# Layer 0 of a four-layer network on one Trainium2 core: one scan of 1024 per pair of states instead of two of 512, and half of softplus's additions as matmuls

## The chip, the cores and the metric

The kernel runs on one core of a Trainium2 chip. Its time is the device time of one execution in microseconds (us), median of several runs; lower is better. The engines of a core work side by side, each on its own queue of instructions in order: TensorE (PE in the profile; PEld is its weight load), VectorE (DVE), ScalarE (ACT), GpSimd (POOL) and SyncE (SP), which here only issues DMAs. They wait for each other through semaphores.

## What is computed

An image batch `x` of 8 x 96 x 64 x 64 (f32) goes through four layers, each `x = x + layer(group_norm(x))`. The change touches the first alone, a selective state space layer (Mamba) over the 4096 pixels of an image, with 192 inner channels and 16 states per channel. The channel flip of the reference leaves the scan itself as it is:

```python
xz = seq @ in_proj_w.T
u, res = jnp.split(xz, 2, axis=-1)
uc = conv_general_dilated(u, conv_w, ...)      # causal, 4 taps, per channel
u = silu(uc)
dbc = u @ x_proj_w.T
dt, B, C = jnp.split(dbc, [DT_RANK, DT_RANK + D_STATE], axis=-1)
delta = softplus(dt @ dt_proj_w.T + dt_proj_b)
dA = exp(delta * A)
dBu = delta * B * u
state_t = dA_t * state_(t-1) + dBu_t           # 192 x 16 states, 4096 steps
y_t = sum over states of state_t * C_t
y = (y + u * D) * silu(res)
out = y @ out_proj_w.T
```

Layer 1 is a Fourier-domain layer, layer 2 a second state space layer (four directions), layer 3 a deformable convolution.

## The kernel before

**Tiling.** `layer0` cuts each image into 8 chunks of NW = 512 pixels, 64 chunks in all. The 192 channels are two halves of HD = 96. A *group* is 32 channels times 4 states on the 128 partitions, and two such sets of states, a *pair*, side by side in one tile of 128 x 2 x 512. A chunk has 12 groups: for each half `h`, six groups `e`. Each takes one *slot* of time `t`; chunk number n starts at slot T = 12 n, and slots are spoken of modulo 12.

**A group's work.** `dd` (delta and delta times u, broadcast by a DMA from SBUF to 128 partitions, six slots ahead, every second group); `da` = exp(delta A) in PSUM tile `ps_d`, two ACT operations of 512 (L405), one slot ahead; `dbu` = (delta u) B on POOL (L424), two slots ahead; the recurrence as `tensor_tensor_scan` on DVE, two of 512 with the starting value from `carry` (L747), in place in `ps_d`; the product with C back into `dbu`, on DVE one slot later (L433); the sum over states by two matmuls into `ps_y` (L444, `total`). For a *late* group the scan writes into `dbu` instead, POOL multiplies by C (L430), and `ps_d` is free as soon as the scan is done; LATE0 names them. After each group ACT copies the last column of both scans into `carry` (L756, `keep`) for the next chunk.

**Order.** `Slots.slot` writes the instruction stream slot by slot. For slot t: the `dd` DMA of t+6; the two exps of t+1; side work marked "first"; the first scan of t; the total of t-2; "pe" side work and the late total of t-4; "act" side work; `dbu` of t+2; "pool" side work; a late product of t-2 on POOL; the product of t-1 on DVE; the second scan of t; then "dve", "sp" and "end" side work. Engines follow that order strictly. Side work is placed by slot number relative to a chunk's T: `sl.at(T - 24, "act", silu)`.

**Side work of a chunk**, before its first group: the convolution as eight matmuls into `ps_a`, one PSUM bank shared by all side matmuls (`inner`, L647); two gate matmuls; four copies to `raw` (L674); one silu over 96 x 2048 with a table load before and one after (L685, L686); `low` (delta's rank, B and C, L691) and its copy; the store of B and C rows to DRAM and their broadcast back, `brep` and `crep`; softplus in `Slots.steps`, as max(x, 0) + log(1 + e) with e = exp(-|x|) and a term for what rounding of 1 + e lost: Abs, Relu, Exp, +1, Ln, -1 on ACT and `add`, `lost`, `delta`, then `delta_u`, on POOL, each over both halves (96 x 1024). After the last group: `y_out`, `gated` (POOL, L798), the output matmuls (L808), the residual as an identity matmul (L815), statistics, store.

**Buffers.** `ps_d` has three buffers of two banks, `ps_y` and `ps_a` one bank each, `dbu` a ring of 7.

Of the kernel before, what the change touches and what calls it, by code (L numbers as in the profile page):

```python
# [39 lines left out]
class Names:  # L40


    def __init__(self):
        self.n = 0
# [271 lines left out]
class Plan:  # L316


    def __init__(self, S):
        self.S, self.plan = S, {}  # L320
# [4 lines left out]
    def put1(self, base, name, i, run):  # L325
        t, engine = PLAN2[name][i]
        self.at(base + t, engine, run)
# [16 lines left out]
class Group:  # L344


    def __init__(self, **kw):
        self.__dict__.update(kw)


class Slots(Plan):
# [14 lines left out]
    def __init__(self, S, consts, pool, psd, ring, red=None):  # L366
        super().__init__(S)
# [22 lines left out]
    def slot(self, t):  # L390
# [19 lines left out]
        if g:  # L410
            g.h = g.dbu if g.late else g.da
            g.scan[0](g.h, g.da, g.dbu)
# [7 lines left out]
        self.side(t, "act")  # L420
        g = G(t + 2)
# [12 lines left out]
        g = G(t)  # L434
        for scan in g.scan[1:] if g else ():
            scan(g.h, g.da, g.dbu)
# [14 lines left out]

    def steps(self, T, out, f, pre, u, reset):


        nc, S, st = self.S.nc, self.S, {}

        def first(h):
            def pe():
                st["p"] = pre(h)

            def act():
                if h == 0:
                    st["e"] = new(f, [HD, 2, NW], "sp_e")
                    st["m"] = new(f, [HD, 2, NW], "sp_m")
                nc.scalar.activation(st["e"][:, h, :], st["p"], AF.Abs)
                nc.scalar.activation(st["m"][:, h, :], st["p"], AF.Relu)

            self.at(T - 20 + h, "pe", pe)
            self.at(T - 19 + h, "first", act)

        first(0)
        first(1)

        def exp():
            nc.scalar.activation(st["e"], st["e"], AF.Exp, scale=-1.0)

        def one():
            st["w"] = new(f, [HD, 2, NW], "sp_w")
            nc.scalar.activation(st["w"], st["e"], AF.Identity, bias=S.one[:HD])

        def ln():
            st["s"] = new(f, [HD, 2, NW], "sp_s")
            nc.scalar.activation(st["s"], st["w"], AF.Ln)

        def less():
            nc.scalar.activation(st["w"], st["w"], AF.Identity, bias=self.minus[:HD])

        for n, run in enumerate((exp, one, ln, less)):
            self.at(T - 18 + n, "act", run)

        def add():
            nc.gpsimd.tensor_tensor(st["m"], st["m"], st["s"], ALU.add)

        def lost():
            nc.gpsimd.tensor_tensor(st["w"], st["w"], st["e"], ALU.subtract)

        def delta():
            out["d"] = new(f, [HD, 2, 2, NW], "delta", bufs=2)
            nc.gpsimd.tensor_tensor(out["d"][:, :, 0, :], st["m"], st["w"], ALU.subtract)

        def delta_u():
            d = out["d"]
            for uv, dv, ov in u(d[:, :, 0, :], d[:, :, 1, :]):
                nc.gpsimd.tensor_tensor(ov, dv, uv, ALU.mult)
            if reset is not None:
                v = d[:, :, 0, :].rearrange("p m (n l) -> p m n l", l=16)
                nc.gpsimd.memset(v[:, :, :, reset : reset + 1], FAR)

        for n, run in enumerate((add, lost, delta, delta_u)):
            self.at(T - 15 + 2 * n, "pool", run)  # L510

# [49 lines left out]
def layer0(S, src, dst, st_in, st_out, images):  # L561
    tc, nc = S.tc, S.nc
    with ExitStack() as ctx:
# [26 lines left out]
        sl = Slots(S, cp, wp, psd, RING0)  # L590
# [48 lines left out]
        def chunk(im, b, c, T):  # L639
            ch, at = {}, c * NW  # L640

            def inner(h, k0, k1):
                def run():
                    if k0 == 0:
                        ch["ps"] = new(psa, [128, NW], "ps_a")
                    for k in range(k0, k1):
                        nc.tensor.matmul(  # L647
                            ch["ps"][:HD, :],
                            wk[:, k, h * HD : (h + 1) * HD],
                            im["xn"][:, at + k : at + k + NW],  # L650
                            start=k == 0,
                            stop=k == 3,
                        )

                return run
# [14 lines left out]
            def raw(n):  # L670
                def run():
                    if n == 0:
                        ch["raw"] = new(fp, [HD, 4, NW], "raw")
                    nc.scalar.activation(  # L674
                        ch["raw"][:, n, :],
                        ch["ps"][:HD, :],
                        AF.Identity,
                        bias=convb[:, n : n + 1] if n < 2 else 0.0,
                    )

                return run

            def silu():
                ch["ug"] = new(fp, [HD, 4, NW], "ug", bufs=4)
                nc.scalar.activation(ch["ug"], ch["raw"], AF.Silu)  # L685
                nc.scalar.preload_act_table_set(LOG_EXP)  # L686
# [16 lines left out]
            sl.at(T - 34, "pe", inner(0, 0, 2))  # L703
            sl.at(T - 33, "pe", inner(0, 2, 4))
            sl.at(T - 32, "first", raw(0))
            sl.at(T - 29, "pe", inner(1, 0, 4))
            sl.at(T - 28, "first", raw(1))
            for h in range(2):
                sl.at(T - 28 + h, "pe", gate(h))
                sl.at(T - 27 + h, "first", raw(2 + h))  # L710
            sl.at(T - 24, "act", silu)
            sl.at(T - 23, "pe", low)
            sl.at(T - 22, "first", low_out)
            sl.at(T - 22, "sp", low_store)

            def pre(h):
                ps = new(psa, [128, NW], "ps_a")
                nc.tensor.matmul(
                    ps[:HD, :],
                    dtw[:, h * HD : (h + 1) * HD],  # L720
                    ch["low"][: RK + 1, :],
                    start=True,
                    stop=True,
                )
                return ps[:HD, :]

            sl.steps(T, ch, fp, pre, lambda d, du: [(ch["ug"][:, 0:2, :], d, du)], None)

            def spread(name, what, t):
# [10 lines left out]
                sl.at(t, "sp", run)  # L740

            spread("b", 0, T - 9)
            spread("c", 1, T - 6)

            def scan_of(n):
                def scan(out, da, dbu, i):
                    nc.vector.tensor_tensor_scan(  # L747
                        out[:, i, :], da[:, i, :], dbu[:, i, :],
                        carry[:, n + i : n + i + 1] if c else 0.0, ALU.mult, ALU.add,
                    )  # L750

                return [lambda *v, i=i: scan(*v, i) for i in range(2)]
# [19 lines left out]
            def y_out(h):  # L772
                def run():
                    if h == 0:
                        ch["yg"] = new(fp, [HD, 2, NW], "yg", bufs=2)
# [7 lines left out]
            for h in range(2):  # L783
                for e in range(NG):
# [6 lines left out]
                        y=y_of(h, e), scan=scan_of(n), late=c % 2 == 0 and NG * h + e in LATE0,  # L791
# [3 lines left out]
                sl.at(T + h * NG + 7, "act", y_out(h))  # L795
# [32 lines left out]
            sl.at(T + 17, "pool", gated)  # L828
            sl.at(T + 17, "sp", residual)
            sl.at(T + 22, "pe", out(0))  # L830
            sl.at(T + 23, "pe", out(1))
            sl.at(T + 23, "pe", plus)
            sl.at(T + 24, "first", sum_out)
            sl.at(T + 25, "dve", stats_out)
            sl.at(T + 25, "sp", store)
# [425 lines left out]
def layer2(S, src, dst, st_in, st_out, images, cp, W, ready, finish):  # L1261
# [3 lines left out]
    with ExitStack() as ctx:  # L1265
# [13 lines left out]
        sl = Slots(S, cp, wp, psd, RING, W["red"])  # L1279
# [383 lines left out]
        def direction(ch, pr, xs, k, n, T):  # L1663
# [49 lines left out]
            for h in range(2):  # L1713
                for i in range(6):
# [6 lines left out]
                        y=y_of(h, e), scan=[scan], late=24 * (n // 2) + 12 * h + e in LATE2,  # L1721
# [636 lines left out]
```

## Time and profile before

| | us |
|---|---|
| three runs | 17171.51, 17232.79, 17279.42 (median 17232.79) |
| profiled execution | 17209.55 |
| its span, first to last instruction | 17207.5 |
| first scan of layer 0 begins | 99.49 |
| last scan of layer 0 begins | 2832.34 |
| first matmul of layer 1 | 2857.52 |

Busy time of the engines over the whole span: DVE 15501.4 us (90%), POOL 14565.0 (85%), PE 14200.8 (83%), ACT 10161.0 (59%). Line numbers (L747) are those of the kernel before. A line of the order-of-time view is: start, length of one record or of several merged, engine, line, operation, tile written and tiles read, shape, count, and in brackets how long the engine stood idle before it and what released it. A line of the waits is: who waited for whom, total us, times, longest.

### The profile page before, as it was taken

The page shows a single profiled execution, that of the slowest core. Times are in us where ns is not written, and L with a number is a line of the kernel's source. Part 1 is how long each engine was busy: PE and PEld are TensorE (multiplying, and loading weights), DVE is VectorE, ACT ScalarE, POOL GpSimd, SP SyncE. Part 2 cuts the span into 40 slices and gives each one's busy share as a digit, 9 for nine tenths or more (in the row PEclk, how much of TensorE's full clock was granted, in tenths as well). Part 3 has the DMA queues.
Part 4 walks back from the last instruction along what each step waited for, and adds up shares of the span by engine and source line. Part 5 has one row for each costly group of instructions (what it writes and reads, how often), then busy time and mean ns, then how long its engine had stood idle before and what let it go on. Part 6 is the DMA issues. An engine that isn't in the chain of part 4 may idle for free.

```text
span 17207.5 us, 127943 instructions
## 1 busy us (share of the span) xinstructions
PE 14200.8 (83%) x36170; PEld 5621.8 (33%) x36170; DVE 15501.4 (90%) x9787; ACT 10161.0 (59%) x15654; POOL 14565.0 (85%) x8237
## 2 busy tenths in 40 slices
PE   8999998979999999999999999999999444444332
PEld 2333334723333333333333333333333111111111
DVE  7999998679999999999999999999999567677677
ACT  7778775557777777777777777777776211111110
POOL 7999995059999999999999999999999556565555
PEclk9999999989999999999999999999999766666666
DMA  5666664366666666666666666666666444454444
GB/s 123 141 136 137 138 137 94 59 167 144 145 142 146 145 140 148 144 141 148 140 144 147 141 145 146 139 147 144 141 147 142 113 140 145 138 150 141 142 126 123
DMA packets 768532, 2373.66 MB, mean 138 GB/s; under 512 B 255989, under 2 KB 257730, under 8 KB 684265
## 3 DMA queue, kind: packets, MB, share of 16 engines
q1 hardware_dynamic: 620361, 1912.33, 50.9%
q0 software_dynamic: 147456, 453.13, 9.0%
q8 instruction: 285, 4.67, 0.1%
q14 instruction: 430, 3.52, 0.1%
HBM read 1249.81 MB, written 108.66 MB: 79 GB/s over the span
## 4 chain that ended last, share of the span: by engine, by line
PE 36%; issue 12%; DVE 11%; another core or an unknown queue 9%; ACT 7%; POOL 5%; DMA 0%; DVEq 0%; SPq 0%; POOLq 0%; ACTq 0%
PE ps_y L444 17%; DVE ps_d L1691 5%; PE ps_a L1342 5%; PE ps_a L1617 4%; ACT ps_d L405 3%; DVE dbu L433 3%; POOL dbu L424 3%; PE ps_a L2022 2%; DVE v L2205 1%; PE ps_a L1433 1%; PE ps_a L1809 1%; DVE s L2214 1%; POOL dbu L430 1%; PE ps_a L1756 1%
## 5 line engine op out<-in xcount | busy, mean ns | idle before, releaser
L424 POOL TENSOR_TENSOR dbu<-dd,brep 128x1024 f32<-128x1024 f32 x3840 | 9060.2, 2418 | 7.2 <-PE ps_y L444 6.9
L444 PE MATMUL ps_y<-dbu,k_red 128*96 128x512 f32 x15360 | 7192.4, 599 | 281.3 <-DVE dbu L433 229.5
L405 ACT ACTIVATE ps_d<-dd,l_alog 128x512 f32<-128x512 f32 x7680 | 5285.2, 691 | 1425.1 <-DVE dbu L433 1010.2
L1691 DVE TENSOR_TENSOR_SCAN ps_d<-ps_d,dbu 128x1024 f32<-128x1024 f32 x2560 | 5829.2, 2285 | 40.5 <-issue 16.4
L433 DVE TENSOR_TENSOR dbu<-ps_d,crep 128x1024 f32<-128x1024 f32 x3296 | 3981.0, 1208 | 0.1
L444 PEld LDWEIGHTS ps_y<-dbu,k_red 128*96 128x96 f32 x15360 | 2444.8, 163 | 4522.4 <-issue 3402.6
L2187 POOL DMA_INDIRECT v<-t,idx x2304 | 2191.8, 951 | 1523.8 <-DVE s L2214 710.2
L2214 DVE TENSOR_REDUCE s<-v 128x864 f32<-128x3456 f32 x256 | 1553.9, 6070 | 402.3 <-remote 293.8
L747 DVE TENSOR_TENSOR_SCAN ps_d<-ps_d,carry,dbu 128x512 f32<-128x512 f32 x1296 | 1610.7, 1279 | 24.1 <-ACT ps_d L405 17.3
L2205 DVE TENSOR_TENSOR v<-v,ps_w 128x3456 f32<-128x3456 f32 x256 | 958.4, 3744 | 679.9 <-ACT ps_w L2197 571.6
L430 POOL TENSOR_TENSOR dbu<-dbu,crep 128x1024 f32<-128x1024 f32 x544 | 1321.2, 2429 | 5.5 <-DVE dbu L1691 3.2
L2233 ACT COPY smp<-ps_t 128x768 f32<-128x768 f32 (+1 forms) x512 | 244.8, 530 | 1635.1 <-remote 929.0
L1691 DVE TENSOR_TENSOR_SCAN dbu<-ps_d,dbu 128x1024 f32<-128x1024 f32 x512 | 1165.2, 2276 | 0.0
L2225 PE MATMUL ps_t<-k_ident,s 128*128 128x128 f32 (+1 forms) x1792 | 328.5, 333 | 971.0 <-issue 660.4
L1342 PE MATMUL ps_a<-pad,woff 96*96 96x512 f32 x2304 | 1046.2, 594 | 4.3 <-ACT pad L1101 1.6
L2022 PE MATMUL ps_a<-xpad,l_om 96*27 96x512 f32 x1152 | 603.0, 674 | 40.0 <-issue 39.9
L2225 PEld LDWEIGHTS ps_t<-k_ident,s 128*128 128x128 f32 (+1 forms) x1792 | 251.4, 170 | 1103.5 <-issue 910.8
L2256 PE MATMUL ps_o<-smp,l_w 128*96 128x512 f32 (+1 forms) x896 | 474.8, 689 | 161.4 <-ACT smp L2233 123.8
L1342 PEld LDWEIGHTS ps_a<-pad,woff 96*96 96x96 f32 x2304 | 376.3, 163 | 623.9 <-issue 583.0
L2039 PE MATMUL ps_u<-k_ident,oc 27*128 27x27 f32 x256 | 33.0, 252 | 629.8 <-ACT oc L2034 486.1
L1160 POOL MEMSET pad<- 96x660 f32 x3 | 1.8, 647 | 611.7 <-DMA y<-yb 611.7
L647 PE MATMUL ps_a<-xn,wk 96*96 96x512 f32 x1024 | 485.5, 607 | 7.0 <-ACT xn L621 2.4
(294 smaller groups left out, 16235.8 us busy)
## 6 DMA issues: line engine op xcount, KB each, us to landing
dd<-delta SPq DMA_DIRECT2D x1920, 512.0 KB
brep<-bcd SPq DMA_DIRECT2D x320, 1024.0 KB
crep<-bcd SPq DMA_DIRECT2D x320, 1024.0 KB
v<-t,idx POOLq DMA_INDIRECT x2304
xl<-x SPq DMA_DIRECT2D x128, 192.0 KB
bcd<-xl SPq DMA_DIRECT2D x64, 256.0 KB
xn<-x SPq DMA_DIRECT2D x64, 192.0 KB
xo<-x SPq DMA_DIRECT2D x64, 192.0 KB
```

The source lines that it names most:

```text
L405: nc.scalar.activation(g.da[:, i, :], g.dd[:, 0, :], AF.Exp, scale=g.a[:, i : i + 1])
L424: nc.gpsimd.tensor_tensor(g.dbu, g.dd[:, 1:2, :].to_broadcast([128, 2, NW]), g.b(), ALU.mult)
L430: nc.gpsimd.tensor_tensor(g.dbu, g.h, g.c(), ALU.mult)
L433: nc.vector.tensor_tensor(g.dbu, g.h, g.c(), ALU.mult)
L444: self.S.nc.tensor.matmul(y, self.red[:, HD - self.gc * (g.n + 1) : 2 * HD - self.gc * (g.n + 1)], g.dbu[:, i, :], start=first and i == 0, ...
L747: nc.vector.tensor_tensor_scan(out[:, i, :], da[:, i, :], dbu[:, i, :], carry[:, n + i : n + i + 1] if c else 0.0, ALU.mult, ALU.add,)
L1342: nc.tensor.matmul(ch["pk"][:HD, :], woff[:, k, m * HD : (m + 1) * HD], pad[:, dy : dy + 8, dx : dx + IW], start=k == 0, stop=k == KT - 1,)
L1691: nc.vector.tensor_tensor_scan(out, da, dbu, 0.0, ALU.mult, ALU.add)
L2022: nc.tensor.matmul(im["pa"][: 3 * KT, :], om[:, k, :], xpad[:, 8 * c + dy : 8 * c + dy + 8, dx : dx + IW], start=k == 0, stop=k == KT - 1,)
L2187: nc.gpsimd.indirect_dma_start(out=st["v"][:, k].rearrange("p q c -> p (q c)"), out_offset=None, in_=flat, in_offset=bass.IndirectOffsetOn ...
L2205: nc.vector.tensor_tensor(v3, v3, ps_w[:, g % 2, j * 4 * KT : (j + 1) * 4 * KT] .unsqueeze(2) .to_broadcast([128, 4 * KT, CH]), ALU.mult,)
L2214: nc.vector.tensor_reduce(st["s"], st["v"].rearrange("p k q c -> p k c q"), mybir.AxisListType.X, ALU.add,)
```

## The change

The pair's two scans become one scan of 1024 over the flattened pair. It carries the first state's last value into the second state's first column, so two one-column operations per group stop that: `join` on ACT adds dA times the second state's carry to the first column of its dBu (`Identity` with a scale and a bias column), one slot ahead and behind "act" work; `cut` on DVE sets the first column of its dA to zero, right ahead of the scan. The first chunk of an image has no carry and no join.

In `Slots`:

```diff
+            if g.cut:
+                g.cut(g.da)
-            g.scan[0](g.h, g.da, g.dbu)
+            g.scan(g.h, g.da, g.dbu)
...
         self.side(t, "act")
+        g = G(t + 1)
+        if g and g.join:
+            g.join(g.da, g.dbu)
...
-        g = G(t)
-        for scan in g.scan[1:] if g else ():
-            scan(g.h, g.da, g.dbu)
```

In `layer0`:

```diff
+            def scan_of(n):
+                def scan(*v):
+                    out, da, dbu = (x.rearrange("p i l -> p (i l)") for x in v)
+                    nc.vector.tensor_tensor_scan(
+                        out, da, dbu, carry[:, n : n + 1] if c else 0.0, ALU.mult, ALU.add
+                    )
+                return scan
+
+            def join_of(n):
+                def join(da, dbu):
+                    b = dbu[:, 1, 0:1]
+                    nc.scalar.activation(
+                        b, da[:, 1, 0:1], AF.Identity, bias=b, scale=carry[:, n + 1 : n + 2]
+                    )
+                return join
+
+            def cut(da):
+                nc.vector.memset(da[:, 1, 0:1], 0.0)
```

Softplus's three additions are split by halves. Half 0 stays on POOL in 96 x 512 operations. For half 1 (HALF holds both chunk parities, so in every chunk) four identity matmuls add the four terms in `ps_a`, and ACT copies the sum out. "-1" becomes 1 - w, so that all are additions. `delta_u` is one POOL operation per half.

```diff
+                def both(i):
+                    def run():
+                        if i == 0:
+                            ch["ps"] = new(psa, [128, NW], "ps_a")
+                        for k, v in enumerate(((e, w), (s, d))[i]):
+                            nc.tensor.matmul(
+                                ch["ps"][:HD, :], S.ident[:HD, :HD], v(),
+                                start=i + k == 0, stop=i + k == 2,
+                            )
...
+                def summed():
+                    nc.scalar.copy(d(), ch["ps"][:HD, :])
...
+                if h and c % 2 in HALF:
+                    put("sums", both(0), both(1), summed)
+                else:
+                    put(f"soft{h}", add, lost, delta)
+                sl.put1(T, "delta_u", h, delta_u)
```

Silu reads the second gate half straight from `ps_a`, so that `raw` has three parts instead of four:

```diff
-                nc.scalar.activation(ch["ug"], ch["raw"], AF.Silu)
+                nc.scalar.activation(ch["ug"][:, 3, :], ch["ps"][:HD, :], AF.Silu)
+                nc.scalar.activation(ch["ug"][:, :3, :], ch["raw"], AF.Silu)
```

The late groups: slot 8 of every other chunk before; now 2 and 7 of even chunks and 2, 7 and 8 of odd ones. All side work gets its places from a table:

```diff
-LATE0 = (8,)
+LATE0 = (2, 7, 14, 19, 20)
+HALF = (0, 1)
...
+PLAN0 = dict(
+    conv0=[(-34, "pe"), (-34, "pe"), (-34, "pe"), (-34, "pe")],
+    conv1=[(-29, "pe"), (-29, "pe"), (-29, "pe"), (-29, "pe")],
+    gate=[(-28, "pe"), (-27, "pe")],
+    raw=[(-32, "first"), (-28, "first"), (-27, "first")],
+    silu=[(-27, "end")],
+    low=[(-23, "pe")],
+    low_out=[(-22, "first")],
+    low_store=[(-15, "sp")],
+    dt=[(-19, "pe"), (-20, "pe")],
+    dt_out=[(-19, "end"), (-19, "first")],
+    exp=[(-17, "act")],
+    one=[(-15, "first")],
+    ln=[(-15, "end")],
+    less=[(-14, "end")],
+    soft0=[(-13, "pool"), (-13, "pool"), (-10, "pool")],
+    soft1=[(-13, "pool"), (-12, "pool"), (-11, "pool")],
+    sums=[(-13, "pe"), (-13, "pe"), (-12, "first")],
+    delta_u=[(-7, "pool"), (-2, "pool")],
+    spread=[(-13, "sp"), (-3, "sp")],
+    y_out=[(7, "end"), (13, "end")],
+    gated=[(20, "pool")],
+    residual=[(16, "sp")],
+    out=[(22, "pe"), (22, "pe")],
+    plus=[(22, "pe")],
+    sum_out=[(22, "end")],
+    stats=[(23, "dve")],
+    store=[(30, "sp")],
+)
```

Before, the same steps lay at: conv -34, -33 and -29; gate -28, -27; raw -32, -28, -27, -26; silu -24 ("act"); low -23; its store -22; dt -20, -19; the softplus steps on ACT one a slot from -18 to -15, on POOL every second slot from -15 to -9; spreads -9 and -6; y_out 7 and 13; gated 17; residual 17; out 22 and 23; store 25. Layer 2 uses the same `Slots`, without join and cut, with its table PLAN2 as it was.

More of the change, by code (lines that the diff above doesn't have):

```diff
@@ L316, with __init__ @@
 class Plan:
-    def __init__(self, S):
-        self.S, self.plan = S, {}
+    def __init__(self, S, table=None):
+        self.S, self.plan, self.table = S, {}, table
     def at(self, t, what, run):
@@ L325, in put1 @@
     def put1(self, base, name, i, run):
-        t, engine = PLAN2[name][i]
+        t, engine = self.table[name][i]
         self.at(base + t, engine, run)
@@ L344 @@
 class Group:
+    join = cut = None
     def __init__(self, **kw):
@@ L351, with __init__ @@
 class Slots(Plan):
-    def __init__(self, S, consts, pool, psd, ring, red=None):
-        super().__init__(S)
+    def __init__(self, S, consts, pool, psd, ring, table, red=None):
+        super().__init__(S, table)
         self.pool, self.psd, self.ring = pool, psd, ring
@@ L450, in total @@
             )
[L452 to L510, printed above, removed]
 class GroupStats:
@@ L589, in layer0 @@
             )
-        sl = Slots(S, cp, wp, psd, RING0)
+        sl = Slots(S, cp, wp, psd, RING0, PLAN0)
         log_exp_tables(S)
@@ L640, in chunk, with conv @@
             ch, at = {}, c * NW
-            def inner(h, k0, k1):
+            def conv(h, k):
                 def run():
-                    if k0 == 0:
+                    if k == 0:
                         ch["ps"] = new(psa, [128, NW], "ps_a")
[L646 to L653, printed above, removed]
+                    nc.tensor.matmul(
+                        ch["ps"][:HD, :],
+                        wk[:, k, h * HD : (h + 1) * HD],
+                        im["xn"][:, at + k : at + k + NW],
+                        start=k == 0,
+                        stop=k == 3,
+                    )
                 return run
@@ L671, in run @@
                 def run():
-                    if n == 0:
-                        ch["raw"] = new(fp, [HD, 4, NW], "raw")
+                    if "raw" not in ch:
+                        ch["raw"] = new(fp, [HD, 3, NW], "raw")
                     nc.scalar.activation(
@@ L701, in low_store @@
                 nc.sync.dma_start(ch["rows"], ch["low"][RK + 1 :, :])
[L703 to L707, printed above, removed]
-            for h in range(2):
[L709 to L723, printed above, removed]
-                )
-                return ps[:HD, :]
-            sl.steps(T, ch, fp, pre, lambda d, du: [(ch["ug"][:, 0:2, :], d, du)], None)
@@ L729, in spread, with put, dt @@
-            def spread(name, what, t):
+            def put(name, *runs):
+                sl.put(T, name, *runs)
+            for h in range(2):
+                put(f"conv{h}", *(conv(h, k) for k in range(4)))
+            put("gate", gate(0), gate(1))
+            put("raw", *map(raw, range(3)))
+            put("silu", silu)
+            put("low", low)
+            put("low_out", low_out)
+            put("low_store", low_store)
+            soft = {}
+            def dt(h):
+                def run():
+                    ch["ps"] = new(psa, [128, NW], "ps_a")
+                    nc.tensor.matmul(
+                        ch["ps"][:HD, :],
+                        dtw[:, h * HD : (h + 1) * HD],
+                        ch["low"][: RK + 1, :],
+                        start=True,
+                        stop=True,
+                    )
+                return run
@@ new lines, in dt_out, with run, exp @@
+            def dt_out(h):
+                def run():
+                    if "e" not in soft:
+                        soft["e"] = new(fp, [HD, 2, NW], "sp_e")
+                        ch["d"] = new(fp, [HD, 2, 2, NW], "delta", bufs=2)
+                    nc.scalar.activation(soft["e"][:, h, :], ch["ps"][:HD, :], AF.Abs)
+                    nc.scalar.activation(ch["d"][:, h, 0, :], ch["ps"][:HD, :], AF.Relu)
+                return run
+            def exp():
+                nc.scalar.activation(soft["e"], soft["e"], AF.Exp, scale=-1.0)
@@ new lines, in one, with ln, less @@
+            def one():
+                soft["w"] = new(fp, [HD, 2, NW], "sp_w")
+                nc.scalar.activation(soft["w"], soft["e"], AF.Identity, bias=S.one[:HD])
+            def ln():
+                soft["s"] = new(fp, [HD, 2, NW], "sp_s")
+                nc.scalar.activation(soft["s"], soft["w"], AF.Ln)
+            def less():
+                nc.scalar.activation(
+                    soft["w"], soft["w"], AF.Identity, bias=S.one[:HD], scale=-1.0
+                )
+            put("dt", dt(0), dt(1))
@@ new lines, in chunk, with half, run, add @@
+            put("dt_out", dt_out(0), dt_out(1))
+            for name, run in (("exp", exp), ("one", one), ("ln", ln), ("less", less)):
+                put(name, run)
+            def half(h):
+                e, w, s = (lambda k=k: soft[k][:, h, :] for k in "ews")
+                d = lambda: ch["d"][:, h, 0, :]
+                def both(i):
+                    def run():
+                        if i == 0:
+                            ch["ps"] = new(psa, [128, NW], "ps_a")
+                        for k, v in enumerate(((e, w), (s, d))[i]):
+                            nc.tensor.matmul(
+                                ch["ps"][:HD, :], S.ident[:HD, :HD], v(),
+                                start=i + k == 0, stop=i + k == 2,
+                            )
+                    return run
+                def summed():
+                    nc.scalar.copy(d(), ch["ps"][:HD, :])
+                def add():
+                    nc.gpsimd.tensor_tensor(d(), d(), s(), ALU.add)
+                def lost():
+                    nc.gpsimd.tensor_tensor(w(), w(), e(), ALU.add)
+                def delta():
+                    nc.gpsimd.tensor_tensor(d(), d(), w(), ALU.add)
+                def delta_u():
+                    nc.gpsimd.tensor_tensor(
+                        ch["d"][:, h, 1, :], d(), ch["ug"][:, h, :], ALU.mult
+                    )
+                if h and c % 2 in HALF:
[3 more added lines that the diff above has]
+                sl.put1(T, "delta_u", h, delta_u)
@@ L730, in run, with spread @@
+            half(0)
+            half(1)
+            def spread(name, what):
                 def run():
@@ L738, in run @@
                     )
-                sl.at(t, "sp", run)
-            spread("b", 0, T - 9)
-            spread("c", 1, T - 6)
+                return run
+            put("spread", spread("b", 0), spread("c", 1))
             def scan_of(n):
-                def scan(out, da, dbu, i):
+                def scan(*v):
+                    out, da, dbu = (x.rearrange("p i l -> p (i l)") for x in v)
                     nc.vector.tensor_tensor_scan(
-                        out[:, i, :], da[:, i, :], dbu[:, i, :],
-                        carry[:, n + i : n + i + 1] if c else 0.0, ALU.mult, ALU.add,
-                    )
-                return [lambda *v, i=i: scan(*v, i) for i in range(2)]
+                        out, da, dbu, carry[:, n : n + 1] if c else 0.0, ALU.mult, ALU.add
+                    )
+                return scan
+            def join_of(n):
+                def join(da, dbu):
+                    b = dbu[:, 1, 0:1]
+                    nc.scalar.activation(
+                        b, da[:, 1, 0:1], AF.Identity, bias=b, scale=carry[:, n + 1 : n + 2]
+                    )
+                return join
+            def cut(da):
+                nc.vector.memset(da[:, 1, 0:1], 0.0)
             def keep(t, n):
@@ L773, in run @@
                 def run():
-                    if h == 0:
+                    if "yg" not in ch:
                         ch["yg"] = new(fp, [HD, 2, NW], "yg", bufs=2)
@@ L790, in chunk @@
                         c=lambda p=part: ch["c"][:, 2 * p : 2 * p + 2, :],
-                        y=y_of(h, e), scan=scan_of(n), late=c % 2 == 0 and NG * h + e in LATE0,
+                        y=y_of(h, e), scan=scan_of(n), join=join_of(n) if c else None, cut=cut, late=12 * (c % 2) + NG * h + e in LATE0,
                     )
@@ L794, in chunk @@
                         sl.at(t + 1, "end", keep(t, n))
-                sl.at(T + h * NG + 7, "act", y_out(h))
+                sl.put1(T, "y_out", h, y_out(h))
             def gated():
@@ L826, in store @@
                 nc.sync.dma_start(dst[b][:, at : at + NW], ch["xo"])
[L828 to L835, printed above, removed]
+            put("gated", gated)
+            put("residual", residual)
+            put("out", out(0), out(1))
+            put("plus", plus)
+            put("sum_out", sum_out)
+            put("stats", stats_out)
+            put("store", store)
             if c == NC - 1:
@@ L1278, in layer2 @@
         dp = ctx.enter_context(tc.tile_pool(name="l2d", bufs=2, space=DRAM))
-        sl = Slots(S, cp, wp, psd, RING, W["red"])
+        sl = Slots(S, cp, wp, psd, RING, PLAN2, W["red"])
         log_exp_tables(S)
@@ L1720, in direction @@
                         c=lambda p=part: dr["c"][:, 2 * p : 2 * p + 2, :],
-                        y=y_of(h, e), scan=[scan], late=24 * (n // 2) + 12 * h + e in LATE2,
+                        y=y_of(h, e), scan=scan, late=24 * (n // 2) + 12 * h + e in LATE2,
                     )
```

## The prediction

> **What bounds the kernel now.** I read the page first: one core, and the edit touches layer 0 only, the first sixth of the span. So the next view is the busy time of each engine in layer 0's steady stretch (columns: stretch, length, then PE, PEld, DVE, ACT, POOL busy and instruction counts, clock, DMA).
>
> ```profile
> 150.00:2750.00 2600.00, 2400.45 (x5296) 816.77 (x5295) 2575.66 (x2295) 2039.36 (x3359) 2474.76 (x1087) 0.98 0.63 138
> ```
>
> DVE is busy 99.1%, POOL 95.2%, PE 92.3%, ACT 78.4%: DVE sets the pace, two others are close. The first scan starts at 99.49 us and the last ends at 2833.6, so a chunk (64 of them, 12 slots each) takes 2734/64 = 42.72 us. Next, the order of time on DVE, and one stretch of layer 2, whose scan already is 1024 long:
>
> ```profile
> 1517.26 2.45 DVE L747 TENSOR_TENSOR_SCAN ps_d<-ps_d,carry,dbu 128x512 f32<-128x512 f32 x2
> 1519.62 1.21 DVE L433 TENSOR_TENSOR dbu<-ps_d,crep 128x1024 f32<-128x1024 f32 x1
> 1520.74 2.46 DVE L747 TENSOR_TENSOR_SCAN ps_d<-ps_d,carry,dbu 128x512 f32<-128x512 f32 x2
> 1523.10 1.21 DVE L433 TENSOR_TENSOR dbu<-ps_d,crep 128x1024 f32<-128x1024 f32 x1
> ...
> 8001.17 2.28 DVE L1691 TENSOR_TENSOR_SCAN ps_d<-ps_d,dbu 128x1024 f32<-128x1024 f32 x1
> 8003.36 1.21 DVE L433 TENSOR_TENSOR dbu<-ps_d,crep 128x1024 f32<-128x1024 f32 x1
> ```
>
> Read starts, not durations: a record overlaps the next by some 0.09 us. Two scans of 512 take 2.36 (1517.26 to 1519.62), the product by C 1.12, one scan of 1024 without carry 2.19. Check: 12 × 2.36 + 11.5 × 1.12 + two bn_stats of 0.58 = 42.4 of 42.72.
>
> Then ScalarE around its longest block, and its waits in 300 to 2500 us:
>
> ```profile
> 1506.39 0.16 ACT L756 COPY carry<-ps_d 128x2 f32<-128x2 f32 x1 [1.61 <-DVE dbu L433]
> 1506.59 1.42 ACT L405 ACTIVATE ps_d<-dd,l_alog 128x512 f32<-128x512 f32 x2
> 1507.98 0.58 ACT L820 COPY xo<-ps_a 96x512 f32<-96x512 f32 x1
> 1508.58 1.28 ACT L685 ACT_TABLE_LOAD   x1
> 1509.87 1.91 ACT L685 ACTIVATE ug<-raw 96x2048 f32<-96x2048 f32 x1
> 1511.80 1.28 ACT L686 ACT_TABLE_LOAD   x1
> 1513.10 0.16 ACT L756 COPY carry<-ps_d 128x2 f32<-128x2 f32 x1
> 1513.29 1.42 ACT L405 ACTIVATE ps_d<-dd,l_alog 128x512 f32<-128x512 f32 x2
> ```
>
> ```profile
> ACT carry L756 <- DVE dbu L433: 196.2, 182, 2.5
> ACT raw L674 <- PE ps_a L647: 94.2, 100, 5.2
> ```
>
> ScalarE runs strictly in order; silu with its two table loads is 4.52 us in one piece. There are three ps_d buffers, so exp(t+1) has to wait until DVE is through with group t-2 (in the trace the carry copy before it waits for that product). In this block ScalarE needs 6.7 us from exp to exp, while DVE has two slots of work in hand (about 7): it just fits, alone in its slot.
>
> **Part by part, per chunk.** DVE: the scan. One of 1024 with a carry is 2.19 + 0.06 (pairs without carry start 1.12 apart, with it 1.18) = 2.25 for 2.36: the merge gains 0.11, not the 0.27 that the durations promise (2 × 1.279 - 2.285). The cut (a one-column memset) is not in the trace in this place. Startup memsets start 0.03 apart; the one-column add at L936 has a record of 0.155. I take 0.05, nearest to the memset, and keep 0.03 to 0.155. Slot: 2.30 + 1.12. Late groups 0.5 to 2.5 per chunk: two products less, 2.24. Sum: 12 × 2.30 + 9.5 × 1.12 + 1.16 = 39.4. DVE alone would gain 3 us.
>
> POOL: a full operation starts every 2.325 (four L424 in 9.30), a 512-wide one every 1.22 (layer 2's L1627, L1630 in order of time). Before: 12 + 0.5 + 4 + 1 = 17.5 full ones, 40.7. After: 12 + 2.5 late + 1 gated = 15.5 full and 5 halves: 36.0 + 6.1 = 42.1, with GroupStats' powers about 42.3. So even if all else fits, the gain stops at 42.3.
>
> PE: records start 0.43 apart, two per matmul; 43 matmuls become 47: 37.0 to 40.4. Not the bound; its conv, low, gate, dt and sums all share one ps_a bank.
>
> SP: the row store goes from T-22 to T-15, past the spreads, dd loads and image loads of seven slots, close before spread b at T-13; spread c to T-3. The rows are ready at T-22 either way and SP's issues take 0.3 to 1.4 us each in the order of time, so I cost it at nothing; the cover is three slots between spread c and its first product at T+1, two for b. Were it gone, a slot's 3.4 us once a chunk.
>
> ACT: added 12 joins, one copy out of PSUM (0.48 from start to start), a second silu (+0.05 net); removed one raw (0.48). The join has two pointer columns. Nearest rows: the carry copy 0.154, gs_ve with one column 0.251, so two make about 0.35, or 0.26 from start to start; bounds 0.15 and 0.36. [...]
>
> What decides is where ACT's work lies. DVE's cut(t+1) waits for join(t+1), which stands on ACT behind exp(t+1) and all "first" and "act" work of slot t. Queued behind the waiting cut: the scan, the products, and so the release of ps_d that exp waits for. And the plan puts raw 2, "one", ln and silu all into slot 9. Let M be the end of product 6 (end of DVE's slot 7), 0.00. From there no DVE work holds ACT up, since group 7 is late and frees ps_d early. ACT by starts: carry 0.03 to 0.22; exp(9) 1.58; raw 1 is held by conv 1, which PE issues after the total that product 5 releases (-3.42 + 1.71 + 3.41 + 0.3 latency, thus 2.0), to 2.58; join 2.84; carry 3.02; exp(10) 4.38; raw 2, behind its gate matmul, 5.03; one 6.08; join 6.34; carry 6.66 (after product 8); ln 7.71; silu 1.29 + 0.48 + 1.50 + 1.30 to 12.28; exp(11) 13.64; join(11) 13.9, with 0.1 of latency 14.0.
> Until then DVE has only slots 8, 9 and 10 to do, 3 × 2.30 + 1.5 × 1.12 = 8.6. It stands still for 5.4 us. After join(11) it has nine slots (11, 0 to 7) at its own pace: 9 × 2.30 + 8 × 1.12 + 1.16 = 30.8. In them ACT keeps up: its heaviest, 5 and 7, need about 3.0 of 3.42. **Period 30.8 + 14.0 = 44.8, 2.1 more than now.**
>
> [...]
>
> Sum: 64 × 2.1 = 134. The last three chunks have no silu to compute for later ones: 3 × -5.4 = -16. Image normalisation puts 0.7 ahead of join(11) in 14 chunks: +10. First chunks have no join: 8 × 3 × -0.26 = -6. Total **+122 us**: 17332 against the profiled execution (17209.55; span 17207.5). That run lies 23 us under the median of 17232.79; on the median 17355. Layers 1 to 3 are unchanged. The mechanism's own bounds: cut 0.03 to 0.155 in nine slots, -12 to +60 us; three joins, about ±20; the wait at raw 1 between nothing and the 0.94 mean of the waits above, -26 to +35. Together about 17300 to 17450.
>
> **Rivals.** *POOL sets the end, slightly faster.* If the stretch from M to join(11) takes under 11.5 us instead of 14.0, DVE's stall disappears behind POOL's 42.3 us: 64 × -0.4 = -27, 17206. At 11.9 it breaks even. For it: POOL's own load is heaviest in slots 8 to 11 too (7.5 to 8.5 full ones, 17 to 20 us), and before, ACT delayed a scan only 15 times in 2200 us. Against: the rows of silu, ln, one and three exps alone make 10.7.
> *One-column operations cost far more.* If the memset into PSUM takes the one-column row's 0.155 and the scan behind it doesn't overlap (0.09), each cut costs 0.2 more: 9 × 0.2 × 64 = +115, 17470. For: no memset into PSUM is in the trace. Against: the aggregate of 0.35 us at 1528.89 holds the next scan for only 0.26.
> *Merge without effect* (2.36 stays) changes 9 × 0.11 × 64 = 63 us, 17418, inside the range.
>
> **How the numbers follow.** A measurement tells about 1% (172 us) from no change here; only layer 0 is touched, so a verdict beyond that needs 2.7 us a chunk. Forecast 0.63, of which 0.12 lies above +172; POOL 0.17; dear columns 0.20 together with the ineffective merge, 0.18 of it beyond +172. Faster by 1% would need a chunk of 40.0, under POOL's 42.3: 0.02. Slower 0.30, within 0.68. The range reaches down to POOL's 17206 and up to the sum of the mechanism's own bounds: 17210 to 17450, leaving out most of dear columns.
>
> **What would show it.** DVE's busy share in 150 to 2750 falls to about 88%, its idle time before the cut or the scan, about 5 us a chunk, ended by ACT, once a chunk, in slots 10 to 11, right after silu. POOL and PE at 94% and 90%. A scan in the 2.3s; joins near 0.35. Wrong if DVE's waits lie in every slot, if POOL is above 99%, or if DVE stays above 95% busy.

## The result and the profile after

| | before | after |
|---|---|---|
| runs, median | 17252.49 us (17171.51 to 17279.42, 4 runs) | 17542.86 us (17525.11 to 17577.63, 4 runs) |
| ratio | | 1.0181, 95% interval 1.0165 to 1.0197: slower |
| profiled execution (span) | 17209.55 (17207.5) | 17577.63 (17575.9) |
| layer 0, first scan to last | 99.49 to 2833.6 | 105.79 to 3145.1 |
| mean chunk (that stretch over 64) | 42.72 | 47.49 |

The loss is layer 0's: 64 x (47.49 - 42.72) = 305 us of stretch, against 290 between the medians. The two profiled executions lie further apart, 368 us between their spans: 311 of it is there by the last scan of layer 0, and 55 lies behind the last scan of layer 2, where the two kernels do not differ. The same stretch of engine busy times as before, in the changed kernel (PE, PEld, DVE, ACT, POOL after the length):

```profile
150.00:2750.00 2600.00, 2396.36 (x5189) 804.80 (x5188) 2214.94 (x1953) 1971.49 (x3650) 2297.38 (x1136) 0.97 0.59 123
```

No engine is full any more: DVE 85.2% (99.1% before), PE 92.2%, POOL 88.4%, ACT 75.8%. So the loss is in waits, and the order of time shows where. DVE from the product of slot 7 on:

```profile
1519.48 1.20 DVE L470 TENSOR_TENSOR dbu<-ps_d,crep 128x1024 f32<-128x1024 f32 x1
1520.69 0.06 DVE L809 MEMSET ps_d<- 128x1 f32 x1
1520.86 2.35 DVE L793 TENSOR_TENSOR_SCAN dbu<-ps_d,carry,dbu 128x1024 f32<-128x1024 f32 x1
...
1526.88 0.06 DVE L809 MEMSET ps_d<- 128x1 f32 x1 [0.82 <-ACT carry L813]
...
1529.31 1.21 DVE L470 TENSOR_TENSOR dbu<-ps_d,crep 128x1024 f32<-128x1024 f32 x1
1534.35 0.06 DVE L809 MEMSET ps_d<- 128x1 f32 x1 [3.84 <-ACT dbu L802]
```

The last line is the cut of group 11: DVE stood still for 3.84 us until ACT's join (L802). From the end of product 6 (1520.68) to this cut is 13.67 us; the mean over chunks 4 to 57 is 14.08. On ACT the same moment:

```profile
1526.46 0.34 ACT L802 ACTIVATE dbu<-ps_d,dbu,carry 128x1 f32<-128x1 f32 x1
1526.70 0.18 ACT L813 COPY carry<-dbu 128x2 f32<-128x2 f32 x1
1526.78 1.06 ACT L721 ACTIVATE sp_s<-sp_w 96x1024 f32<-96x1024 f32 x1
1527.86 1.28 ACT L657 ACT_TABLE_LOAD   x1
1529.15 0.59 ACT L657 ACTIVATE ug<-ps_a 96x512 f32<-96x512 f32 x1
1529.65 1.47 ACT L658 ACTIVATE ug<-raw 96x1536 f32<-96x1536 f32 x1
1531.13 1.28 ACT L659 ACT_TABLE_LOAD   x1
1532.42 1.41 ACT L437 ACTIVATE ps_d<-dd,l_alog 128x512 f32<-128x512 f32 x2
1533.93 0.35 ACT L802 ACTIVATE dbu<-ps_d,dbu,carry 128x1 f32<-128x1 f32 x1
```

From join 10 (1526.46) to join 11 (1533.93) nothing waits; ACT simply works through ln, table load, silu, table load and exp, 7.5 us, while DVE had a scan and a product to do.

Two things in the first fence were not forecast in their size. The product takes its whole 1.21 us to the next start (1.12 before, without a memset behind it), and the scan starts 0.17 us after a memset of 0.06. And a second wait, of about 1 us, lies at slots 2 to 3. DVE and then ACT, in the chunk where it can be read best:

```profile
1685.17 2.35 DVE L793 TENSOR_TENSOR_SCAN dbu<-ps_d,carry,dbu 128x1024 f32<-128x1024 f32 x1
1687.44 1.20 DVE L470 TENSOR_TENSOR dbu<-ps_d,crep 128x1024 f32<-128x1024 f32 x1
1689.88 0.06 DVE L809 MEMSET ps_d<- 128x1 f32 x1 [1.25 <-ACT carry L813]
```

```profile
1683.40 0.58 ACT L833 COPY yg<-ps_y 96x512 f32<-96x512 f32 x1
1685.04 0.16 ACT L813 COPY carry<-ps_d 128x2 f32<-128x2 f32 x1 [1.05 <-DVE dbu L470]
1687.56 1.42 ACT L437 ACTIVATE ps_d<-dd,l_alog 128x512 f32<-128x512 f32 x2 [2.36 <-DVE dbu L793]
1689.48 0.34 ACT L802 ACTIVATE dbu<-ps_d,dbu,carry 128x1 f32<-128x1 f32 x1
```

The scan is that of group 2, a late group. The exp of group 3 (1687.56) waits 2.36 us until that scan ends (1687.52); join 3 (1689.48) stands behind the exp, and the cut of group 3 (1689.88) waits for the join. This tie of exp 3 to scan 2 comes from a buffer. A late group's `ps_d` is free as soon as its scan is done, and in the program as built (there it is settled which buffer a group gets) group 3 has just this buffer in 48 of the 64 chunks; in the others it has that of group 0, whose product ended 2.5 us earlier (1685.0 here). The times fit: in 40 of the chunks 4 to 57 exp 3 starts within 0.1 us after the end of scan 2, and DVE then stands still for 1.15 us on the average before cut 3; in the other 14 it stands still for 0.01. In other chunks ACT's copy of the last output (L833) waits too, for totals on TensorE; here it waits for nothing, and DVE stands still all the same.

The mean idle time of DVE by place, worked out from its order of time (chunks 4 to 59; even / odd chunks; 0.1 is the gap inside each cut, memset to scan):

```
                 slot 2 to 3     8 to 9      9 to 10     10 to 11    all 12
before           0.00 / 0.00   0.00 / 0.00  0.05 / 0.00  0.00 / 0.00   0.43
after            1.21 / 0.73   0.50 / 0.56  0.11 / 0.92  4.22 / 3.90   7.06
```

### The profile page after: what moved, and what is told of

Its sections match the earlier page's. It is cut to its first block, busy times and chain, and to the rows that moved or that the text cites. A ratio compares the mean times of both kernels' runs of the same rounds, so it can differ in the third digit from the quotient of the medians.

```text
span 17575.9 us, 129658 instructions
## 1 busy us (share of the span) xinstructions
PE 14478.5 (82%) x36682; PEld 5708.7 (32%) x36682; DVE 15388.0 (88%) x9659; ACT 10317.5 (59%) x16390; POOL 14654.2 (83%) x8429
## 4 chain that ended last, share of the span: by engine, by line
PE 33%; issue 11%; another core or an unknown queue 10%; DVE 9%; POOL 7%; ACT 7%; DMA 0%; DVEq 0%; SPq 0%; POOLq 0%; ACTq 0%
PE ps_y L478 16%; PE ps_a L1398 5%; DVE ps_d L1747 4%; POOL dbu L461 4%; PE ps_a L1673 4%; ACT ps_d L437 3%; DVE dbu L470 3%; PE ps_a L2078 2%; PE ps_a L1865 1%; POOL dbu L467 1%; PE ps_a L1489 1%; POOL v L2243 1%; DVE v L2261 1%; DVE s L2270 1%
## 5 line engine op out<-in xcount | busy, mean ns | idle before, releaser
L470 DVE TENSOR_TENSOR dbu<-ps_d,crep 128x1024 f32<-128x1024 f32 x3168 | 3813.8, 1204 | 0.0
L467 POOL TENSOR_TENSOR dbu<-dbu,crep 128x1024 f32<-128x1024 f32 x672 | 1614.4, 2402 | 118.0 <-ACT carry L813 88.0
L793 DVE TENSOR_TENSOR_SCAN ps_d<-ps_d,carry,dbu 128x1024 f32<-128x1024 f32 x528 | 1244.8, 2358 | 57.6 <-DVE ps_d L809 1.8
```

Of the source, the lines that this page charges most:

```text
L467: nc.gpsimd.tensor_tensor(g.dbu, g.h, g.c(), ALU.mult)
L470: nc.vector.tensor_tensor(g.dbu, g.h, g.c(), ALU.mult)
L793: nc.vector.tensor_tensor_scan(out, da, dbu, carry[:, n : n + 1] if c else 0.0, ALU.mult, ALU.add)
```

## The experiments

All are read by the mean chunk of layer 0, since everything after it is the same. All but e7 (4 runs) and e8 (10 runs) are single executions. The first four ran on a chip on which the kernel before takes 16408.20 us; there the granted clock from 13000 us on, mostly layer 3, is 0.80 instead of 0.71, so totals are not compared across the two. Layer 0 is unmoved by it: the run without a cut is 237 us over that chip's before, and 64 x (46.19 - 42.72) = 222.

| run | mean chunk, us | in all, against the kernel before on its chip |
|---|---|---|
| before | 42.72 | |
| after | 47.49 | 17542.86 / 17252.49 |
| e1_no_cut | 46.19 | 16645.47 / 16408.20 |
| e2_cut_aside | 46.06 | 16640.90 / 16408.20 |
| e3_spread | 47.70 | 16747.67 / 16408.20 |
| e4_two_scans | 45.15 | 16583.28 / 16408.20 |
| e5_merge_alone | 47.95 | 17584.04 / 17256.17 |
| e6_no_tables | 45.18 | 17423.64 / 17256.17 |
| e7_old_places | 44.69 | 17379.97 / 17256.17 |
| e8_one_late | 42.03 | 17220.67 / 17256.17 |
| e9_old_places_pool | 42.39 | 17247.74 / 17236.39 |
| e10_no_half | 46.61 | 17469.15 / 17236.39 |

**The cut left out (e1), and the cut elsewhere (e2).**

```diff
-  ... join=join_of(n) if c else None, cut=cut, ...
+  ... join=join_of(n) if c else None, ...
```
```diff
-                nc.vector.memset(da[:, 1, 0:1], 0.0)
+                nc.vector.memset(aside, 0.0)
```

> The memset that cuts the two states apart is left out, so the second state starts from the first one's end; all else is the changed kernel. Measured by the mean chunk of layer 0 (first scan to last, over 64; 47.5 us in the changed kernel, 42.7 before). Theory (the block on ScalarE from product 6 to join 11, 14.1 us, plus a cut that costs VectorE 0.25 in each slot): only the nine slots outside the block gain, 9 x 0.25 = 2.2, so 45.2, with the block still 14 us. Rival 1 (the cut costs its 0.06 us record): 47.0. Rival 2 (the waits for ScalarE in every slot are what grew): block and rest shrink together, below 44.

> The same memset of one column per group, written to a column in SBUF that nothing reads; the states are not cut apart, as in the run without it. If the 0.25 us is the price of a small instruction as such, the chunk stays at 47.5 us. If it is the price of writing PSUM and of the scan's wait for that write, the chunk comes out near 45.4 us (the run without a cut plus 12 starts of about 0.03) and the scan starts 0.03 to 0.06 after the memset instead of 0.165.

Measured: 46.19 and 46.06. DVE's order of time in the second:

```profile
1501.83 1.20 DVE L470 TENSOR_TENSOR dbu<-ps_d,crep 128x1024 f32<-128x1024 f32 x1
1502.96 2.34 DVE L794 TENSOR_TENSOR_SCAN dbu<-ps_d,carry,dbu 128x1024 f32<-128x1024 f32 x1
1502.98 0.06 DVE L810 MEMSET aside<- 128x1 f32 x1
```

Product to scan is 1.13 us here, 1.38 in the changed kernel (1519.48 to 1520.86): the cut costs 0.25 us in a slot without waits, and the same memset into a column that nobody waits for costs nothing that the slots show. So in these runs it is not the small instruction as such that is dear, but the write to `ps_d` with a scan behind it that reads what was just written. The rows part the price into 0.09 ahead of the memset (it starts only when the product has ended) and 0.165 from its start to the scan's; which cause stands behind either part these runs leave open, since e2 changes both. The chunk falls by 1.3 and 1.4, not by 2.2, a miss for both expectations: DVE's idle time, freed of the cut's own 1.3, rises from 5.8 to 7.4 in e1. A part of the cut lay in the shadow of other waits. The block from product 6 to join 11 stays (14.4 in e1), so the waits are not made by the cut.

**Steps moved out of silu's slot (e3).**

```diff
-    exp=[(-17, "act")],
-    one=[(-15, "first")],
-    ln=[(-15, "end")],
+    exp=[(-18, "act")],
+    one=[(-17, "act")],
+    ln=[(-14, "end")],
     less=[(-14, "end")],
```

> Three of softplus's steps leave the silu's slot: exp at -18, one at -17, ln and less at -14; all else is the changed kernel. Theory: the block from product 6 to join 11 loses one (1.05) and ln (0.95), from 14.1 to 12.1 us, so the chunk falls by 2.0 to 45.5 us; a little more if PE's wait for less also eases. Rival (GpSimd sets the end, or the cut alone): no change, 47.3 to 47.6.

Measured 47.70: a miss, no gain. The block shrank from 14.1 to 13.7 in the mean, not to 12.1. ACT's order of time there, exp(10) first:

```profile
1722.47 1.42 ACT L437 ACTIVATE ps_d<-dd,l_alog 128x512 f32<-128x512 f32 x2
1725.01 0.59 ACT L646 ACTIVATE raw<-ps_a 96x512 f32<-96x512 f32 x1 [1.12 <-PE ps_a L632]
...
1726.83 1.28 ACT L657 ACT_TABLE_LOAD   x1 [0.91 <-PE ps_a L632]
```

The two steps are gone and ACT waits 2.0 us in their place, for the two gate matmuls (L632). PE reaches these late: conv 1, the diagonal product and the total of group 6 come first, and each gate needs the single bank `ps_a` that `raw` has to clear. So two chains of nearly equal length end at the silu, ACT's work and the exchange of `ps_a` with PE, and ln and one had lain in the shadow of the second. What was left over (ln and less now run behind join 11) went into new idle time of DVE at slot 11 to 12, 0.8 in even and 0.4 us in odd chunks.

**No silu, no table loads (e6).** It leaves silu out of both halves, u and gate.

```diff
-  nc.scalar.activation(ch["ug"][:, 3, :], ch["ps"][:HD, :], AF.Silu)
-  nc.scalar.activation(ch["ug"][:, :3, :], ch["raw"], AF.Silu)
-  nc.scalar.preload_act_table_set(LOG_EXP)
+  nc.scalar.activation(ch["ug"][:, 3, :], ch["ps"][:HD, :], AF.Identity)
+  nc.scalar.activation(ch["ug"][:, :3, :], ch["raw"], AF.Identity)
```

> The changed kernel with Identity in place of silu and without the two table loads, so silu is left out: 2.57 us less on ScalarE, all of it behind the last wait for TensorE in the block. Theory after the spread run (ln and one lay in the shadow of TensorE's chain through ps_a, but what follows the silu's start is bare): the block falls from 14.1 to 11.5 and the chunk by 2.6, to 44.9 us. Rival (something other than ScalarE's order holds join 11, such as GpSimd or a DMA): under 1 us of change.

Measured: block 11.29, chunk 45.18, idle time at slot 10 to 11 down from 4.2 / 3.9 to 1.5 / 1.2. That is close to what was expected: ACT's 2.57 us less took 2.8 out of the block, so what follows the gates on ACT is bare there, and no transfer or GpSimd holds join 11. The chunk fell by 2.3, since the wait at slots 2 to 3 rose to 1.2 / 1.2.

**The merge undone (e4), and the merge alone (e5).** In e4 two scans of 512 stand again on both sides of the product, without join and cut; in e5 the kernel before gets the one scan, the join and the cut and nothing else.

> Only the merge is undone: two scans of 512 in the order of before, no join, no cut; the plan, the late groups and the softplus half on TensorE stay. Theory: VectorE's slot goes from 3.65 back to 3.48, and the block loses three joins and ends at the first of two exps (14.1 to about 12.5), while exp may start one scan earlier: a chunk of 43 to 44 us, still above 42.7 for the silu's slot. Rival 1 (the new places and the softplus half are the whole loss): 46 us or more. Rival 2 (the merge is the whole loss): GpSimd's 42.3 or below before's 42.7.

> The kernel before with nothing but the merge: one scan of 1024, join and cut; places, late group and softplus as before. If the merge is a loss by itself: VectorE's work is 12 x 2.44 + 11.5 x 1.21 + 1.2 = 44.3 us a chunk, and the silu, now ahead of a join in slot 0, stops it for some 3 us more: 46.5 to 47.7 us (before 42.7). If the merge gains what the scan rows promise, 42 or below; if the merge needs the new places to pay, between the two.

Measured 45.15 and 47.95, each above its expected range. In the changed kernel the merge costs 47.49 - 45.15 = 2.3 us a chunk; in the places of before it costs 5.2, more than the whole change. There the idle time (2.5 / 3.8 us) follows slot 0, where silu stands ahead of a join. So the new places did ease the merge, and still not enough. e4 came out 1 us above its expectation: the wait at slot 10 to 11 stayed at 4.2 / 4.1 us without any join. It belongs to the silu's place, not to the merge. e4 also shows the tie of exp 3 to scan 2 by itself: its program has it in 24 of 64 chunks, and where exp 3 starts right after scan 2 (21 of the chunks 4 to 57) DVE stands still for 1.54 us, in the other 33 for 0.00.

**The softplus half (e7, e9, e10).** e7: two scans, the steps near the places of before, the half on TensorE, late groups 2 and 8. e9 is e7 with that half back on GpSimd and late group 8 alone; e10 is the changed kernel with it back on GpSimd:

```diff
-HALF = (0, 1)
+HALF = ()
```

> Two scans as before, the steps near the places of before (silu alone in slot 0, sums in slot 11), the softplus half on TensorE, and late groups 2 and 8 in every chunk; no join, no cut. By the sums of rows: VectorE 12 x 2.36 + 10 x 1.12 + 1.2 = 40.7, TensorE 40.4, GpSimd 15 x 2.325 + 5 x 1.22 + 0.2 = 41.2: a chunk of 41.3 to 42.2 us, 30 to 90 us faster than before in all. If the softplus half itself is what hurts (TensorE's chain through ps_a), 43 or more.

> The old-places kernel of the last call (44.7 us a chunk) with the whole of softplus's additions back on GpSimd (six operations of 96 x 512) and late group 8 in every chunk, so that four matmuls and one copy a chunk are gone; nothing else. GpSimd: 14 x 2.325 + 8 x 1.22 + 0.2 = 42.5, VectorE 41.8. If the softplus half on TensorE caused that kernel's waits (ScalarE's raw and output copies for TensorE), the chunk falls to 42.5 to 42.9. If the moved statistics, out and normalisation steps caused them, it stays above 44.

> The changed kernel with softplus's second half back on GpSimd in its three places; merge, places and late groups stay. GpSimd's work becomes 14.5 + 1 full operations and 8 of 512, 36.0 + 9.8 + 0.2 = 46.0 us a chunk. Theory: VectorE's wait of about 1.0 us at slot 2 to 3 (the copy of the last output waits for totals that stand behind the sums on TensorE) goes away, the wait after the silu's block stays at 4, and the chunk is 46.2 to 46.8. Rival (slot 2 waits for something else, or GpSimd's added 3.7 us turn into waits): 47.5 or more, with the wait at slot 2 unchanged.

e7 missed: 44.69 instead of 41.3 to 42.2 (ratio to before 1.0066, 1.0045 to 1.0087). All sums of work said 41.2 and less. The waits in 300 to 2500 us of e7, and then of e9:

```profile
ACT raw L649 <- PE ps_a L622: 210.6, 61, 4.6
ACT yg L835 <- PE ps_y L481: 153.1, 98, 3.8
```

```profile
ACT raw L649 <- PE ps_a L622: 50.3, 92, 1.4
ACT yg L835 <- PE ps_y L481: 17.3, 41, 0.9
```

With the half back on GpSimd ACT's waits for TensorE fall from 364 to 68 us and the chunk to 42.39, just under the expected 42.5; the moved statistics, out and normalisation steps are in both, so they are not the loss. But these waits of ACT are not what most of the loss came through. DVE stands still for 3.56 us a chunk in e7 and 0.51 in e9, and 1.5 of that lies before group 9, behind late group 8:

```profile
1663.25 1.28 DVE L794 TENSOR_TENSOR_SCAN dbu<-ps_d,carry,dbu 128x512 f32<-128x512 f32 x1
1666.06 2.62 DVE L794 TENSOR_TENSOR_SCAN ps_d<-ps_d,carry,dbu 128x512 f32<-128x512 f32 x2 [1.54 <-ACT ps_d L437]
```

```profile
1664.56 1.41 ACT L437 ACTIVATE ps_d<-dd,l_alog 128x512 f32<-128x512 f32 x2 [3.82 <-DVE dbu L794]
```

It is the tie of the changed kernel again: exp 9 starts when scan 8 ends (1664.53), in 46 of the chunks 4 to 57, and each time DVE then waits 1.54 us. As built, group 9 has late group 8's buffer in 55 of 64 chunks of e7 and in none of e9. The rest of the difference (0.6 us before group 2, 0.5 before group 10, little elsewhere) may come from TensorE's queue; as late group 2 goes with the half, the two are not parted.

In the changed kernel, e10 is faster by 0.9 us a chunk, though GpSimd gets 3.7 more to do: 46.61, as expected, with DVE's idle time at slot 2 to 3 down from 1.21 / 0.73 to the 0.1 of the cut and that after the silu unchanged (4.2 / 3.9). The reason is another than the expected one: as built, e10 gives group 3 the buffer of group 0 in every chunk, and its exp 3 starts before scan 2 has ended throughout. Moving the half thus brought the tie; why the buffers are then given out differently is not shown. GpSimd is 97.5% busy in e10, so 46.61 is also near the least that its 46.0 us of work allow.

**One late group in every chunk (e8).**

```diff
-  ... late=c % 2 == 0 and NG * h + e in LATE0,
+  ... late=NG * h + e in LATE0,
```

> The kernel before with its late group 8 in every chunk instead of every other one; nothing else. VectorE loses half a product, 0.56 us, GpSimd gains 1.16: 41.8 and 42.0 us; a chunk of 42.0 to 42.5, 15 to 45 us faster in all. If GpSimd's waits add to its work, no change.

Measured: 17220.67 us (10 runs) against 17256.17 (13 runs), ratio 0.9981, 95% interval 0.9970 to 0.9992, chunk 42.03. As expected, and a little faster than the kernel before. It leaves little room for another step of this kind:

```profile
150.00:2750.00 2600.00, 2403.78 (x5354) 822.92 (x5353) 2585.95 (x2301) 2054.42 (x3401) 2583.05 (x1134) 0.98 0.64 140
```

DVE (third pair) is busy 99.5%, GpSimd (fifth) 99.3%: both are full.

## Why the prediction was wrong

The sign and the main mechanism held; the size did not, and the time lies above the range. (The bounds that the prediction lists add up to 17297 to 17470, not to 17450; 17542.86 lies above that too.)

- **The block on ACT**: forecast 14.0 us from product 6 to join 11, measured 14.08; forecast once a chunk at slots 10 to 11, ended by ACT, 5.4 us of idle DVE; measured 4.1 there and, without the cuts' own gaps, another 0.4 in even and 1.3 in odd chunks at slots 8 to 10. e6 shows that ACT's work there is the cause. Part of the working was lucky: ln and one stood in the sum as work, and e3 shows that the exchange of `ps_a` with PE would have filled most of that time anyway. Its 0.3 us of latency ahead of raw 1 and 0.1 behind join 11 stand in no row; they were the author's estimate. Measured over chunks 4 to 57, raw 1 starts 2.02 us after product 6 in the mean (forecast 2.0), and cut 11 0.07 us (median) after the end of join 11.
- **The cut, the term that was most mis-sized**: "I take 0.05, nearest to the memset, and keep 0.03 to 0.155". It costs 0.25, outside both bounds. The record is 0.059, as in startup; what I left out is that the product before it no longer overlaps (0.09) and that the scan waits for it (0.165 from start to start). Over the nine slots outside the block, 9 x 0.20 x 64 = 115 us. The rival "one-column operations cost far more" had this price, 0.2 more per cut, though its record is 0.059 and not 0.155, and was given a fifth together with the ineffective merge; it was true beside the forecast, not instead of it. Taking the two as alternatives kept their sum, some 17470, out of the range.
- **The nine slots after join 11, where a wait was missing**: "In them ACT keeps up", and before it "There are three ps_d buffers, so exp(t+1) has to wait until DVE is through with group t-2". A late group counted only as one that frees `ps_d` early. But in three of four chunks exp 3 waits for the scan of group 2, right before it, and DVE waits for exp 3: 0.86 us a chunk (the mean of the two idle times at slot 2 to 3, less the cut's 0.11), 55 us in all. e10, which has no such tie, is 0.88 us a chunk faster. "Not the bound", said of PE, stood: busy 92.2% for the forecast 90%.
- In the trace that is the whole miss: the block took 14.08 us for 14.0, the rest of the period 33.4 for 30.8, and 9 x 0.20 + 0.86 = 2.7. In all, 122 + 115 + 55 = 292 us, for 290 measured. That it closes so well is partly luck: leaving the cut out (e1) gave back 1.3 us a chunk and not 9 x 0.25 = 2.2, since other waits took its place.
- **Right**: the merge gains next to nothing in scan time (2.27 from start to start, forecast 2.25); the join (0.342, forecast 0.35); the table loads (1.29 us from the first load to silu and 1.29 from the second to exp, forecast 1.29 and 1.30).
- **Rivals**: GpSimd as the bound falls, at 88.4% busy, with e10 faster although it gives it more. "Merge without effect" (2.36 stays) falls with the scan's 2.27; what e5 shows is that join and cut cost more than the scan gains.

On the cut, the trace of the changed kernel shows a wait for VectorE's own semaphore between the memset and the scan, 768 times for 768 scans, and the scan starts 0.163 us after the memset in the median (mean 0.170). Where no cut stands between the two, products of 1.21 us are followed by the next scan after 1.12 (before) and 1.13 (e2).

## What to carry to other kernels

Cost a helper instruction between two long dependent ones by the distance of its neighbours' starts with and without it, not by its record: 0.06 us of memset was 0.25 us of engine. Where a buffer is freed early, look which work gets it next: in e7 group 9 got that of group 8, and DVE waited 1.54 us for it. Sums of work do not show this; they gave e7 41.2 us and the chip 44.7. When in-order engines feed each other, add up the stretch between two points where one must wait for the other; that sum was right to 0.1 us, with the luck said above, where shares of busy time said nothing.

## What was not expected of the hardware

In the changed kernel a memset of one column into `ps_d`, between a product and the scan that reads the column, held back its neighbours by four times its record (0.25 us for 0.06), while in e2 one into SBUF that nothing reads ran beside the scan (1502.98 against 1502.96). And the cut that cost 0.25 us a slot gave back only 1.3 us a chunk when it was left out.
